# Transposing half of layer 1's rows in 32x32 blocks on VectorE, with a trip through DRAM, in place of TensorE

## The chip, the cores and the metric

One Trainium2 chip, one core. The metric is the device time of one execution in microseconds (us). The kernel before took 974.26 us (median of 3 runs, 972.87 to 974.94).

## The reference

The kernel computes two graph layers on 4096 rows of 512 numbers. Cut to what matters here:

```python
# layer 0: attention inside 32 graphs of 128 rows; adj is both bias and edge encoding
h = jnp.maximum(_layernorm(x, axis=-1), 0.0)
x = x + _L0_gnn_ref(h, adj, adj, ptr, Wq, bq, Wk, bk, Wv, bv)
# layer 1: graph attention over all 4096 rows, 8 heads of 64
h = jnp.maximum(_layernorm(x, axis=-1), 0.0)
mx = jnp.einsum('nf,hfd->hnd', h, W)          # projection
...
attn = jax.nn.softmax(jnp.where(adj[None] > 0, logits, neg_inf), axis=-1)
out_h = jnp.einsum('hij,hjd->hid', attn, mx)  # aggregation
x = x + ...
```

The change touches the rows of layer 1 between the norm and the projection. The projection needs each row tile (128 rows) transposed.

## The kernel before

Layer 0 writes its rows to `x1_d` in DRAM. For each of 32 row tiles, layer 1 loads the rows, norms them, transposes them with four TensorE matmuls, puts them through relu and projects them. Then it aggregates over all tiles with the masks in `a_d`.

```python
def norm(src, hn):
    nc.vector.bn_stats(stats, src)
    nc.vector.bn_aggr(mv, stats)
    nc.gpsimd.tensor_scalar(ve, mv[:, 1:2], EPS, None, ALU.add)
    nc.gpsimd.tensor_tensor(rstd, ve, neghalf, ALU.pow)                # L120
    nc.vector.tensor_scalar(hn, src, mv[:, 0:1], rstd, ALU.subtract, ALU.mult)   # L121

def relu_T(ps_pool, hn, dst):
    for k in range(KC):
        nc.tensor.transpose(pt[:, k, :], hn[:, ts(k, P)], ident)       # L127
    nc.scalar.activation(dst, pt, AF.Relu)                             # L128
...
def normed1(i):
    row = sb2.tile([P, D], F32, name="row1")
    nc.sync.dma_start(row, x1_d[i])
    norm(row, row)
    hT = sb2.tile([P, KC, P], F32, name="hT1")
    relu_T(ps_t, row, hT)
    return hT

def prepare(i, hT, part):
    pm = project1(ps_p, hT, w1x)                                       # L243, pp
    e = sb2.tile([P, EW], F32, name="e")
    nc.scalar.activation(e[:, ES:EC], pm[1][:, HW : HW + H], AF.Exp)
    weigh(e, pm)                                                       # L252, VectorE, frees PSUM
    split(e, part)                                                     # L231, GpSimd
...
for i in range(n - 1, NT):
    hT = nhT
    if i + 1 < NT:
        nhT = normed1(i + 1)
    prepare(i, hT, part_tile(lo if i < LO else hi, i))
# then, for every tile: mw load (L265), VectorE transpose (L270) and cast (L277) of the mask,
# and the aggregation pg (L283). After tile 1's: graphs_are_tiles (the check of ptr) and hold(...).
```

Some words used below: relu is max(x, 0). The *weighing* (`weigh`) multiplies the projected rows by e and so empties their PSUM tile. A *hand-off* is a point where one engine waits for a result of another. The *granted clock* is the share of its full speed that TensorE was given.

The order of each engine's instructions is fixed when the kernel is compiled, and it isn't the order of the program: the prediction names a mask load issued 127 us ahead of its use.

## Time and profile before

| | before |
|---|---|
| time, median | 974.26 us |
| span of the profiled execution | 970.5 us, granted clock 0.992 |
| projection of tile 5 starts (from about here on layer 1's rows set TensorE's pace) | 351.77 us |
| projection of tile 16 (the first that the change turns) | 405.14 us |
| aggregation (pg) starts | 468.74 us |
| aggregation lasts | 489.6 us |

I cut the stage at the starts of the projections of tiles 5 and 16 and of pg, read from TensorE's timeline. The *first stretch* (tile 5 to tile 16) takes 405.14 - 351.77 = 53.4 us, the *second* (tile 16 to pg) 468.74 - 405.14 = 63.6 us. The same cut is made for every kernel below. The profile lines of this kernel stand in the prediction.

### The profile page before, as it was taken

The page shows a single profiled execution, that of the slowest core. Times are in us where ns is not written, and L with a number is a line of the kernel's source. Part 1 is how long each engine was busy: PE and PEld are TensorE (multiplying, and loading weights), DVE is VectorE, ACT ScalarE, POOL GpSimd, SP SyncE. Part 2 cuts the span into 40 slices and gives each one's busy share as a digit, 9 for nine tenths or more (in the row PEclk, how much of TensorE's full clock was granted, in tenths as well). Part 3 has the DMA queues.
Part 4 walks back from the last instruction along what each step waited for, and adds up shares of the span by engine and source line. Part 5 has one row for each costly group of instructions (what it writes and reads, how often), then busy time and mean ns, then how long its engine had stood idle before and what let it go on. Part 6 is the DMA issues. An engine that isn't in the chain of part 4 may idle for free.

```text
span 970.5 us, 13180 instructions
## 1 busy us (share of the span) xinstructions
PE 940.3 (97%) x5051; PEld 817.5 (84%) x5051; DVE 459.4 (47%) x978; ACT 260.7 (27%) x505; POOL 184.0 (19%) x344
## 2 busy tenths in 40 slices
PE   8999999989999998999999999999999999999995
PEld 5676677766677776788999999999999999999994
DVE  4678777866766358655133242433424233242321
ACT  5865666665762222233100000000000000000000
POOL 2211113231122125555110110101011010110100
PEclk9999999999999999999999999999999999999998
DMA  9989889898883033221022312223131221312201
GB/s 343 419 346 378 322 329 364 355 369 317 336 339 148 33 104 108 72 66 55 1 76 56 88 50 82 62 69 87 44 87 52 80 85 47 87 49 82 61 27 37
DMA packets 58042, 148.28 MB, mean 153 GB/s; under 512 B 6386, under 2 KB 23026, under 8 KB 49778
## 3 DMA queue, kind: packets, MB, share of 16 engines
q1 hardware_dynamic: 48178, 130.31, 38.3%
q10 hardware_dynamic: 9792, 17.05, 4.6%
q8 instruction: 41, 0.67, 0.3%
q14 instruction: 31, 0.25, 0.1%
HBM read 113.77 MB, written 33.55 MB: 152 GB/s over the span
## 4 chain that ended last, share of the span: by engine, by line
PE 89%; DVE 3%; DMA 2%; POOL 2%; ACT 2%; issue 1%; SPq 0%; ACTq 0%; DVEq 0%; POOLq 0%
PE pg L283 50%; PE pp L420 11%; PE pp L408 10%; PE pp L243 9%; PE pp L493 3%; PE pss L466 3%; PE pt L127 2%; DMA row<-x_d 1%; POOL part L231 1%; DMA xg<-x 1%; DVE a L136 1%; ACT junk L443 1%; DVE row L121 0%; DVE stats L114 0%; POOL rstd L120 0%
## 5 line engine op out<-in xcount | busy, mean ns | idle before, releaser
L283 PE MATMUL pg<-part,at 128*128 128x348 f32 x3072 | 489.6, 321 | 1.2 <-DVE e L252 1.2
L283 PEld LDWEIGHTS pg<-part,at 128*128 128x128 f32 x3072 | 489.4, 188 | 1.5 <-issue 1.5
L277 DVE CAST at<-at 128x4096 fp32r<-128x4096 fp8e4 x32 | 74.0, 2313 | 312.2 <-PE pg L283 312.2
L290 ACT COPY tot<-pg 128x522 f32<-128x522 f32 x32 | 19.2, 599 | 470.5 <-PE pg L283 470.5
L443 ACT ACTIVATE junk<-a 128x2048 bf16<-128x2048 f32 (+15 forms) x92 | 124.4, 1352 | 48.7 <-DVE x L495 28.0
L243 PE MATMUL pp<-w1x,hT 128*128 128x256 f32 (+1 forms) x512 | 118.4, 385 | 0.0
L420 PE MATMUL pp<-wv,hT 128*128 128x512 f32 x256 | 116.6, 600 | 0.0
L408 PE MATMUL pp<-hT,m_sb 128*128 128x256 f32 x512 | 113.2, 379 | 0.0
L243 PEld LDWEIGHTS pp<-w1x,hT 128*128 128x128 f32 x512 | 95.7, 192 | 13.6
L408 PEld LDWEIGHTS pp<-hT,m_sb 128*128 128x128 f32 x512 | 96.1, 190 | 12.9 <-issue 0.5
L420 PEld LDWEIGHTS pp<-wv,hT 128*128 128x128 f32 x256 | 49.1, 192 | 61.9 <-issue 61.9
L136 DVE TENSOR_SCALAR a<-a 128x512 fp8e4<-128x512 f32 x256 | 98.2, 460 | 0.5 <-DMA a_d<-a 0.4
L595 POOL COPY den_all<-tot 128x1 f32<-128x1 f32 x31 | 5.8, 186 | 369.1 <-DVE tot L291 369.1
L128 ACT ACTIVATE hT<-pt 128x512 f32<-128x512 f32 x64 | 37.0, 598 | 68.8 <-PE pt L127 68.7
L604 POOL TENSOR_TENSOR tot<-tot,row 128x512 f32<-128x512 f32 x31 | 40.0, 1290 | 61.7 <-DVE tot L296 61.7
L231 POOL TENSOR_TENSOR part<-e,part 128x522 fp32r<-128x522 f32 x32 | 42.1, 1316 | 43.0 <-ACT part L230 38.8
L118 POOL TENSOR_SCALAR ve<-mv 128x1 f32<-128x1 f32 x64 | 18.7, 295 | 150.9 <-DVE mv L116 150.8
L252 DVE TENSOR_TENSOR e<-pp,e 128x256 f32<-128x256 f32 x64 | 26.6, 417 | 28.9 <-ACT e L371 25.2
L270 DVE STREAM_TRANSPOSE at<-mw 128x1024 f32<-128x1024 f32 x32 | 39.5, 1236 | 0.0
L120 POOL TENSOR_TENSOR rstd<-ve,neghalf 128x1 f32<-128x1 f32 x64 | 38.5, 604 | 4.4
L424 DVE TENSOR_TENSOR v<-pp,bv_sb 128x512 f32<-128x512 f32 x32 | 22.0, 688 | 36.0 <-PE pp L420 36.0
L412 ACT ACTIVATE gT<-pp,c_sb 128x256 f32<-128x256 f32 x64 | 29.7, 468 | 29.4 <-PE pp L408 29.3
(93 smaller groups left out, 584.1 us busy)
## 6 DMA issues: line engine op xcount, KB each, us to landing
a<-adj SPq DMA_DIRECT2D x64, 1024.0 KB, 13.1
a_d<-a SPq DMA_DIRECT2D x32, 512.0 KB, 10.6
row<-x_d SPq DMA_DIRECT2D x64, 256.0 KB, 3.5
mw<-a_d SPq DMA_DIRECT2D x128, 128.0 KB, 4.0
xg<-x SPq DMA_DIRECT2D x16, 512.0 KB, 4.7
x_d<-x ACTq DMA_DIRECT2D x32, 256.0 KB, 4.2
out<-tot ACTq DMA_DIRECT2D x31, 256.0 KB, 3.8
wkT_sb<-wkT SPq DMA_DIRECT2D x4, 256.0 KB, 6.3
```

The source lines that it names most:

```text
L120: nc.gpsimd.tensor_tensor(rstd, ve, neghalf, ALU.pow)
L128: nc.scalar.activation(dst, pt, AF.Relu)
L136: nc.vector.tensor_scalar(a8v[:, u], av[:, u], 0.0, None, ALU.is_gt, saturate=False)
L231: nc.gpsimd.tensor_sub(dst[:, :, 1, :], e3, dst[:, :, 0, :].bitcast(F32))
L243: nc.tensor.matmul(pm[g][:, :n], hT[:, k, :], w1x[:, k, g * HW : g * HW + n], start=(k == 0), stop=(k == KC - 1),)
L270: nc.vector.transpose(at8.rearrange("p c n b -> p (c n b)").bitcast(F32).rearrange("p (c u n) -> p c u n", c=NW, n=B), mw.rearrange("p u ( ...
L277: nc.vector.tensor_copy(at.rearrange("p (c b) q -> p c b q", b=BY), at8.rearrange("p c q b -> p c b q"))
L283: nc.tensor.matmul(pg[:, c, : 2 * CW1], at[:, j, :], part(j)[:, c].rearrange("p s w -> p (s w)"), start=(j == 0), stop=(j == NT - 1),)
L408: nc.tensor.matmul(pp[:, : G * P], m_sb[:, k, ts(m, P)], hT[:, k, :], start=(k == 0), stop=(k == KC - 1),)
L420: nc.tensor.matmul(pp, hT[:, k, ts(t, P)], wv[:, k, :], start=(k == 0), stop=(k == KC - 1))
L443: nc.scalar.activation(junk[:, c0:c1], a[:, c0:c1], AF.Exp, scale=2.0 * NEG, accum_out=sums[:, n : n + 1],)
L604: nc.gpsimd.tensor_add(num, num, row)
```

## The change

The intent is to take the transposes of tiles 16 to 31 off TensorE, which is full there. VectorE can transpose 32x32 blocks in SBUF, and it has time. The blocks then have to change partition groups. That is done by a write to DRAM and a read-back (the *trip*), four row tiles (a *group*) at a time. I call the norm, relu and block transpose of such a row its *turning*, and the number of tiles by which the program places it before its projection the *lead* (AHEAD). Cut to its core:

```diff
+MIXED = NT // 2
+AHEAD = 7
+    hT_d = dram.tile([NW, P, P // B, KC * P], F32, name="hT_d")
...
-        ptr_i = sb.tile([1, NPTR], I32, name="ptr_i", bufs=1)
+        ptr_i = sb.tile([1, NPTR], I32, name="ptr_i", tag="row3", bufs=1)
...
+            sb4 = prep.enter_context(
+                tc.tile_pool(name="sb4p", bufs=2, side="right", reuse_waits="tile")
+            )
+            def turn1(i):
+                row = sb4.tile([P, D], F32, name="row4", bufs=4)
+                nc.sync.dma_start(row, x1_d[i])
+                norm(row, row)
+                nc.scalar.activation(row, row, AF.Relu)
+                c, b = divmod(i, BY)
+                if b == 0:
+                    blocks[c] = sb4.tile([P, P // B, KC, BY, B], F32, name="blocks")
+                nc.vector.transpose(
+                    blocks[c][:, :, :, b], row.rearrange("p (k q f) -> p q k f", k=KC, f=B)
+                )
+                if b == BY - 1:
+                    nc.scalar.dma_start(hT_d[c], blocks[c].rearrange("p q k b r -> p q (k b r)"))
+                    hT = sb4.tile([P, P // B, KC, P], F32, name="hT4")
+                    for q in range(P // B):
+                        nc.sync.dma_start(
+                            hT[ts(q, B)].rearrange("p u k m -> p u (k m)"),
+                            hT_d[c, :, q].rearrange("(u f) w -> f u w", f=B),
+                        )
+                    mixed[c] = hT
...
             for i in range(len(ahead) - 1, NT):
+                if MIXED <= i + AHEAD < NT:
+                    turn1(i + AHEAD)
+                j = i + 1
+                if j < MIXED:
+                    hTs[j] = normed1(j)
+                hT = hTs[i] if i < MIXED else mixed[i // BY][:, i % BY]
                 prepare(i, hT, part_tile(lo if i < LO else hi, i))
```

The block trip mixes the rows of a group of four tiles, so half of the mask bytes of layer 0 are laid out in another order to match (one rearrange pattern), and so is the slow fallback path, which doesn't run here. The new buffer of ptr_i comes with the change: it makes the check of the pointer wait for row3, which is first used in the aggregation.

More of the change, by code (lines that the diff above doesn't have):

```diff
@@ L133, in mask_bytes @@
         a8v = a8.rearrange("p (u c q b) -> p u c b q", c=NW, q=B, b=BY)[:, :, half]
-        av = a.rearrange("p (c b u q) -> p u c b q", c=NW // 2, b=BY, q=B)
+        order = ("p (c b u q) -> p u c b q", "p (c u b q) -> p u c b q")[h]
+        av = a.rearrange(order, c=NW // 2, b=BY, q=B)
         for u in range(P // B):
@@ L566 @@
             )
-            n = len(ahead)
-            nhT = ahead[-1]
-            for i in range(n - 1, NT):
-                hT = nhT
-                if i + 1 < NT:
-                    nhT = normed1(i + 1)
+            sb4 = prep.enter_context(
+                tc.tile_pool(name="sb4p", bufs=2, side="right", reuse_waits="tile")
+            )
+            blocks, mixed = {}, {}
+            def turn1(i):
[18 more added lines that the diff above has]
+                    mixed[c] = hT
+            hTs = {len(ahead) - 1: ahead[-1]}
+            for i in range(len(ahead) - 1, NT):
+                if MIXED <= i + AHEAD < NT:
[4 more added lines that the diff above has]
+                hT = hTs[i] if i < MIXED else mixed[i // BY][:, i % BY]
                 prepare(i, hT, part_tile(lo if i < LO else hi, i))
@@ L828, with level_rows @@
                     tc.tile_pool(name="ps_m4", bufs=2, space=PSUM) as ps_m,
-                    tc.For_i(0, NT, 1) as i,
                 ):
-                    hT = sb.tile([P, KC, P], F32, name="hT1")
-                    row = load_row(sb, i)
-                    norm(row, row)
-                    relu_T(ps_t, row, hT)
-                    pm = project1(ps_m, hT, w1x)
-                    te = small.tile([P, H], F32, name="te")
-                    nc.vector.tensor_tensor(te, pm[1][:, HW : HW + H], shift, ALU.subtract)
-                    nc.vector.tensor_scalar(te, te, 0.0, None, ALU.min)
-                    e = sb.tile([P, EW], F32, name="e")
-                    nc.gpsimd.memset(e[:, EC:], 1.0)
-                    nc.scalar.activation(e[:, ES:EC], te, AF.Exp)
-                    weigh(e, pm)
-                    split(e, parts_e[:, ds(i, 1)].rearrange("p o c s w -> p (o c) s w"))
+                    def level_rows(i, row):
+                        hT = sb.tile([P, KC, P], F32, name="hT1")
+                        norm(row, row)
+                        relu_T(ps_t, row, hT)
+                        pm = project1(ps_m, hT, w1x)
+                        te = small.tile([P, H], F32, name="te")
+                        nc.vector.tensor_tensor(te, pm[1][:, HW : HW + H], shift, ALU.subtract)
+                        nc.vector.tensor_scalar(te, te, 0.0, None, ALU.min)
+                        e = sb.tile([P, EW], F32, name="e")
+                        nc.gpsimd.memset(e[:, EC:], 1.0)
+                        nc.scalar.activation(e[:, ES:EC], te, AF.Exp)
+                        weigh(e, pm)
+                        split(e, parts_e[:, ds(i, 1)].rearrange("p o c s w -> p (o c) s w"))
+                    with tc.For_i(0, MIXED, 1) as i:
+                        level_rows(i, load_row(sb, i))
+                    with tc.For_i(MIXED, NT, BY) as i:
+                        for u in range(BY):
+                            row = sb.tile([P, D], F32, name="row1")
+                            for b in range(BY):
+                                nc.sync.dma_start(
+                                    row[ts(b, B)],
+                                    x1_d[ds(i + b, 1), ts(u, B)].rearrange("o p d -> (o p) d"),
+                                )
+                            level_rows(i + u, row)
                 with (
```

## The prediction

> **What bounds the kernel now.** I read the page first: its chain of work that ended last, then the busy tenths, then windows over the stage that the change touches, the timeline of that stage, and its waits.
>
> ```profile
> PE 89%; DVE 3%; DMA 2%; POOL 2%; ACT 2%; issue 1%; SPq 0%; ACTq 0%; DVEq 0%; POOLq 0%
> ...
> L283 PE MATMUL pg<-part,at 128*128 128x348 f32 x3072 | 489.6, 321 | 1.2 <-DVE e L252 1.2
> ```
>
> TensorE carries 89% of the chain. Its largest group, the aggregation of layer 1 (pg), starts at 468.7 us and runs 489.6 us with an idle time of 1.2 us before it. The change removes nothing there. What it touches is the stage before: each of 32 row tiles of layer 1 is normed (VectorE, GpSimd), transposed by four TensorE matmuls into pt, passed through relu (ScalarE) and projected with w1x (pp, line 243). Counted from their starts in the timeline, tiles 16 to 31 are projected from about 404.5 us on, so I cut the stage there. Columns of the windows: stretch, its length, then busy time (instructions) of PE, weight loads, VectorE, ScalarE, GpSimd, then clock, DMA share and GB/s.
>
> ```profile
> 356.00:404.50 48.50, 42.92 (x200) 35.07 (x200) 37.90 (x76) 13.21 (x31) 26.08 (x48) 0.96 0.35 98
> 404.50:468.70 64.20, 63.06 (x318) 54.49 (x316) 33.92 (x79) 20.18 (x48) 34.52 (x75) 1.00 0.18 54
> ```
>
> In the second stretch TensorE is full (63.06 of 64.20) and VectorE has nearly half its time free. In the first, TensorE misses 5.6 us and VectorE is at 37.9 of 48.5. The timeline of TensorE in the full stretch (start, length, engine, line, count) gives the period:
>
> ```profile
> 448.11 0.60 PE L127 MATMUL pt<-ident,row 128*128 128x128 f32 x4
> 448.55 3.67 PE L243 MATMUL pp<-w1x,hT 128*128 128x264 f32 x16
> 452.06 0.60 PE L127 MATMUL pt<-ident,row 128*128 128x128 f32 x4
> 452.49 3.67 PE L243 MATMUL pp<-w1x,hT 128*128 128x264 f32 x16
> ```
>
> Start to start a tile takes 452.49 - 448.55 = 3.94 us: 3.51 of projection and 0.44 of transposes (448.55 - 448.11). The lengths overlap, so I use starts. The waits of TensorE from 350 to 475 us (waiter, released by: us, times, longest):
>
> ```profile
> PE pt L127 <- DVE row L121: 5.6, 4, 3.0
> PE pg L283 <- DVE e L252: 1.2, 1, 1.2
> ```
>
> So the only named waits are for a normed row, in the first stretch, and one for the last PSUM reader before the aggregation.
>
> **What the Trainium skill says.** "VectorE: DVE Perf Modes", section "The three transpose paths": VectorE only transposes 32x32 blocks and TensorE is the path for a whole 128x128. That is why the changed kernel needs a trip through DRAM to move blocks between partition groups. The kernel before already does this for the masks; its transposes of 128x1024 take 1236 ns (row below). "DMA: Bandwidth & Descriptors", section "Anatomy of one DMA" gives a fixed part of about 2.0 us and then bytes over 436 GB/s. That fit is for software-generated transfers; still, the shortest row load here takes 2.0 us and the median in this stage 2.6 us for 256 KB, close to its 2.6. The same page, "Two DMAs through the same engine are not ordered": a read of what another DMA wrote has to wait for its semaphore. So write and read-back add up; no run yet shows it for this pair. "SBUF — State Buffer", section "SBUF: two separate sides": VectorE and GpSimd can lock each other out of a shared port for a whole instruction. The trace agrees in kind: the norm of a row (L121) normally takes 0.55 us, but 1.44 us at 398.83, beside a GpSimd subtraction.
>
> **The change part by part.** The costs come from these groups (busy us, mean ns) and transfers (count, KB each, us to landing):
>
> ```profile
> L128 ACT ACTIVATE hT<-pt 128x512 f32<-128x512 f32 x64 | 37.0, 598 | 68.8 <-PE pt L127 68.7
> L252 DVE TENSOR_TENSOR e<-pp,e 128x256 f32<-128x256 f32 x64 | 26.6, 417 | 28.9 <-ACT e L371 25.2
> L270 DVE STREAM_TRANSPOSE at<-mw 128x1024 f32<-128x1024 f32 x32 | 39.5, 1236 | 0.0
> L120 POOL TENSOR_TENSOR rstd<-ve,neghalf 128x1 f32<-128x1 f32 x64 | 38.5, 604 | 4.4
> ...
> row<-x_d SPq DMA_DIRECT2D x64, 256.0 KB, 3.5
> mw<-a_d SPq DMA_DIRECT2D x128, 128.0 KB, 4.0
> wv<-wvT SPq DMA_DIRECT2D x1, 1024.0 KB, 7.4
> ```
>
> Removed: the transposes of 16 tiles on TensorE, 16 x 0.44 = 7.0 us, all in the stretch where TensorE is full. Busy time would say 64 matmuls x 0.28 = 18 us, or 10 us with their overlap taken out, but most of that is pipeline depth. Relu stays on ScalarE, from SBUF instead of PSUM; a 128x522 copy from SBUF takes 0.62 us against 0.60, so 16 times nothing.
>
> Added on VectorE: 16 transposes of 128x512, half of 1236 ns each, 16 x 0.62 = 9.9 us. Per tile VectorE does 0.69 + 0.18 (statistics) + 0.55 (norm) + 2 x 0.42 (weighing) = 2.26 us now. In the iterations that prepare tiles 16 to 24 it does 2.26 + 0.62 = 2.9 us within 3.51, so it fits. In iterations 9 to 15 it norms two tiles, 2 x 1.42 + 0.62 + 0.84 = 4.3 us against 3.94: over by 7 x 0.36 = 2.5 us. But this is the stretch where VectorE now also does other work. The check of the graph pointer (lines 304 to 330) takes 0.83 + 8 x 0.82 + 1.0 = 8.4 us, and three transposes and two casts of layer 1's masks take 3.7 + 5.2 = 8.9 us. The change puts ptr_i in the buffer of row3, which comes free only inside the aggregation, where VectorE is about 31% busy. The turning buffers (4 x 2 + 2 x 8 + 2 x 8 = 40 KB per partition) lie on the side where the mask buffers come next, which pushes those casts back too. So up to 17 us of VectorE work leaves the stretch and 7 to 10 turnings of 2.04 us come in. I book that as even.
>
> Added transfers: 4 writes of 1 MB and 16 reads of 256 KB, 8 MB in some 100 us, beside a DMA share of 0.18 to 0.35. Bandwidth is free; latency counts. For the last tile of a group: row load 2.6, norm 0.69 + 0.18 + 0.22 + 0.60 + 0.55 plus hand-offs of about 0.5 = 2.7, relu 0.6, transpose 0.62, write of 1 MB about 7 (the loads of 1 MB took 7.4 and 6.9), four reads together about 6 (estimate from 1 MB): 19.5 us. Its place in the program is four tiles ahead of the first use, 4 x 3.94 = 15.8 us or later 4 x 3.51 = 14.0 us. Taken in program order each group would be 4 to 5.5 us late. But the kernel before does not keep program order: the first mask loads of the aggregation are issued at 342.02 us, 127 us before their matmul, as soon as memory allows. The last rows of x1 leave for DRAM at 367.1 us, those of tiles 16 to 24 long before, and the turning needs only free buffers (four rows, two blocks). So I expect it to be drawn ahead by some tiles, and the groups to arrive mostly in time. I book 2 us of lateness in all.
>
> The switch into the aggregation keeps its 1.2 us; the first mask cast (2.3 us) has VectorE to itself in the last seven tiles, where only weighing is left. I book 0. The block order of half the mask bytes in layer 0 changes only strides, with runs of 32 floats as before: 0.
>
> Sum: -7.0 + 0 + 2 + 0 = -5 us; with a share of the 5.6 us of waits in the first stretch perhaps recovered, -6 us. 974.3 - 6 = 968 us.
>
> **Rivals.** *First, late groups.* The reads of a group wait on the SyncE queue for the write; any row load issued behind them waits too. For: that queue issues in order, the chain above is longer than its four tiles, and a late row blocks VectorE and then the weighing that frees PSUM. Against: the order is not the program's, and three of the four groups have rows loaded well ahead. With 5 us a group it makes 974 - 7 + 20 = 987 us; with rows blocked behind as well, about 1000. *Second, VectorE becomes the bound* in iterations 9 to 15, with the waits for GpSimd and ScalarE inside each norm in its order. For: it is at 37.9 of 48.5 there and TensorE already waits 5.6 us. Against: the pointer check moves out. It makes 972 to 980. *Third, more gain:* the moved pointer check and casts free the first stretch and its 5.6 us vanish with the 7.0: 961 to 963. *Fourth,* the first mask cast stands between the stages, since its buffers overlap the turning's: 2 to 6 us more, 970 to 974.
>
> **Range and chances.** The gain is capped: 7.0 + 5.6 = 12.6 us is 1.3%, so over 2% (19.5 us) faster needs something I do not see: 0.03. Over 2% slower needs 26 us of new waits, the strong form of the first rival: 0.10. The rest, 0.87, is within. The range goes from just below the third rival, 960, to a mild form of the first, 982; its upper side is longer because every surprise but one costs time.
>
> **What would show it.** Right: TensorE transposes of rows halve to 64; tiles 16 to 31 follow each other every 3.51 us; VectorE has 16 transposes of about 620 ns; the pointer check lies after 480 us; the aggregation starts some 6 us earlier and still takes 489 to 490 us. Wrong: TensorE waiting, every fourth tile, for a read of the turned rows (first rival); waits for the normed row above 8 us before tile 16 (second); a gap over 3 us before pg with a cast in it (fourth); transposes well over 620 ns, or writes over 10 us.

## The result, and the profile after

| | before | after |
|---|---|---|
| time, median of 6 runs | 973.04 us (972.23 to 974.94) | 984.65 us (983.46 to 988.76) |
| ratio of the fast runs | 1 | 1.0125 [1.0101, 1.0148] |
| profiled span, clock | 970.5 us, 0.992 | 981.6 us, 0.986 |

The kernel became 1.25% slower. That is inside the class "within 2%", but outside the range of 960 to 982, and the sign is wrong. Ratios here and below are the mean time of one kernel's fast runs over that of the other's fast runs of the same rounds, so not quite the ratio of the medians quoted.

Where the 11.1 us between the two profiled spans lie (starts read from TensorE's timeline; differences taken before rounding):

| part | before | after | difference |
|---|---|---|---|
| up to the projection of tile 5 | 351.8 | 351.0 | -0.8 |
| first stretch | 53.4 | 55.4 | +2.1 |
| second stretch | 63.6 | 73.05 | +9.5 |
| aggregation | 489.6 | 491.8 | +2.2 |
| rest | 12.2 | 10.3 | -1.9 |

The page of the kernel after, answering to the first two lines shown of before (chain by engine, and the aggregation's group):

```profile
PE 86%; DVE 5%; DMA 5%; POOL 2%; ACT 1%; issue 1%; SPq 0%; ACTq 0%; POOLq 0%; DVEq 0%
...
L288 PE MATMUL pg<-part,at 128*128 128x348 f32 x3072 | 491.8, 322 | 7.5 <-DVE at L282 7.5
```

TensorE's share of the chain fell, and VectorE and DMA now stand in it with 5% each. The aggregation waits 7.5 us for a mask cast where it waited 1.2 us. TensorE's waits in the stage (us, times, longest), after:

```profile
PE pg L288 <- DVE at L282: 7.5, 1, 7.5
PE pp L248 <- DMA hT<-hT_d: 7.4, 1, 7.4
PE pt L131 <- DVE row L125: 6.8, 4, 2.7
```

Before, there were 5.6 us for rows and 1.2 us ahead of pg. The two windows, after (the second runs to the new start of pg; columns as in the prediction):

```profile
356.00:404.50 48.50, 41.67 (x185) 33.74 (x184) 35.23 (x73) 15.30 (x34) 24.96 (x57) 0.93 0.44 134
404.50:479.50 75.00, 60.09 (x266) 51.25 (x265) 37.71 (x77) 18.51 (x43) 32.89 (x68) 0.93 0.42 114
```

Look at VectorE, the fifth figure. In the first window it is busy 35.2 us; before it was 37.9. So the busy time did come out even, as booked, and slightly better (over the whole first stretch 37.6 us after and 41.0 before). Yet TensorE ran 185 matmuls where it had run 200. TensorE's timeline shows how (start, length, engine, line, count, and the idle time before with its releaser):

```profile
369.82 3.67 PE L248 MATMUL pp<-w1x,hT 128*128 128x264 f32 x16
...
374.82 3.67 PE L248 MATMUL pp<-w1x,hT 128*128 128x264 f32 x16
380.80 1.12 PE L131 MATMUL pt<-ident,row 128*128 128x128 f32 x4 [2.31 <-DVE row L125]
381.71 4.78 PE L248 MATMUL pp<-w1x,hT 128*128 128x264 f32 x16
...
397.89 36.77 PE L248 MATMUL pp<-w1x,hT 128*128 128x264 f32 x160
442.05 29.93 PE L248 MATMUL pp<-w1x,hT 128*128 128x264 f32 x128 [7.39 <-DMA hT<-hT_d]
479.50 0.92 PE L288 MATMUL pg<-part,at 128*128 128x348 f32 x2 [7.52 <-DVE at L282]
```

The starts of the projections lie 374.82 - 369.82 = 5.0 us and 381.71 - 374.82 = 6.9 us apart instead of 3.94: tile by tile TensorE waits for a normed row. Part of the 6.9 us is a slower clock: the projection at 381.71 took 4.78 us instead of 3.67, and the granted clock was 0.52 from 382 to 384 us. After the wait of 2.71 us that ends at 397.25 it was 0.50 from 398 to 400 us. Later TensorE runs without transposes, ten tiles in one piece (160 matmuls) and then eight (128), but there is a hole between them, and another before pg.

**What VectorE does in a 5 us tile.** Its timeline, after:

```profile
371.75 0.66 DVE L118 BATCH_NORM_STATS2 stats<-row 128x6 f32<-128x512 f32 x1
372.83 1.44 DVE L125 TENSOR_SCALAR row<-row,mv,rstd 128x512 f32<-128x512 f32 x1 [0.42 <-POOL rstd L124]
...
375.36 0.55 DVE L125 TENSOR_SCALAR row<-row,mv,rstd 128x512 f32<-128x512 f32 x1 [1.00 <-POOL rstd L124]
375.82 0.42 DVE L257 TENSOR_TENSOR e<-pp,e 128x256 f32<-128x256 f32 x1
376.60 0.71 DVE L588 STREAM_TRANSPOSE blocks<-row 128x512 f32<-128x512 f32 x1 [0.36 <-ACT row L584]
```

and GpSimd's line of the same moment:

```profile
372.76 1.23 POOL L236 TENSOR_TENSOR part<-e,part 128x522 fp32r<-128x522 f32 x1
```

Two norms stand one after the other, one for TensorE's next tile and one for a turned tile. Each waits for GpSimd's rstd (0.42 and 1.00 us), and the first takes 1.44 us instead of 0.55 while GpSimd's split of 1.23 us runs beside it. Then the transpose waits 0.36 us for ScalarE's relu. None of these waits is long, but each holds up the whole list. From 350 to 410 us the norm's groups (busy us, mean ns, idle before) read, before:

```profile
L121 DVE TENSOR_SCALAR row<-row,mv,rstd 128x512 f32<-128x512 f32 x10 | 8.1, 805 | 7.4 <-POOL rstd L120 7.4
```

and after:

```profile
L125 DVE TENSOR_SCALAR row<-row,mv,rstd 128x512 f32<-128x512 f32 x15 | 12.5, 830 | 9.1 <-POOL rstd L124 6.7 <-POOL e L375 2.2
L588 DVE STREAM_TRANSPOSE blocks<-row 128x512 f32<-128x512 f32 x8 | 5.5, 695 | 1.1 <-ACT row L584 1.1
```

**The hole at 442.** The third group (tiles 24 to 27) is written, and read back, at these issue times of the ScalarE and SyncE queues:

```profile
429.07 0.36 ACTq L592 DMA_DIRECT2D hT_d<-blocks  x1
```

```profile
434.25 1.75 SPq L595 DMA_DIRECT2D hT<-hT_d  x4
```

From the write's issue to TensorE's start on it are 442.05 - 429.07 = 13.0 us. TensorE had finished the tiles before at 434.66 (397.89 + 36.77). So the last transpose of this group would have had to be done some 7 us earlier. Nothing of this group's last three rows had been drawn ahead: their loads were issued by 409.1 us and took at most 7.2 us, but VectorE began the first of them only at 419.56 and the last at 423.65 us, when TensorE was in tile 20, which is the last row's place in the program. From 412 to 419 us VectorE had only weighings in its list and waited 1.6 us for ScalarE before two of them. The fourth group, written at 442.26, was in time, but its read-back was issued only at 446.17; without this hole it would have been wanted near 434.66 + 4 x 3.51 = 448.7 us, so it probably owes its punctuality to the hole.

**The hole before pg.** VectorE's last steps, after:

```profile
472.37 0.18 DVE L313 CAST ends<-ends_i 1x64 f32<-1x64 int32 x1
...
475.46 0.42 DVE L624 TENSOR_REDUCE held<-ok 128x1 f32<-128x256 f32 x1
475.79 1.23 DVE L275 STREAM_TRANSPOSE at<-mw 128x1024 f32<-128x1024 f32 x1
477.06 2.29 DVE L282 CAST at<-at 128x4096 fp32r<-128x4096 fp8e4 x1
```

The last weighing, which starts at 472.02, ends about where this cut begins. After it come 475.79 - 472.37 = 3.4 us of checks (all but the first 0.1 us are the bound checks of `hold`) and then 1.23 + 2.29 us for the first mask, which in the kernel before was cast at 361.22 us. Its loads were issued at 342.02 us before and from 448.41 us on now.

### The profile page after: what moved, and what is told of

Its sections match the earlier page's. It is cut to its first block, busy times and chain, and to the rows that moved or that the text cites. A ratio compares the mean times of both kernels' runs of the same rounds, so it can differ in the third digit from the quotient of the medians.

```text
span 981.6 us, 13107 instructions
## 1 busy us (share of the span) xinstructions
PE 937.6 (96%) x4987; PEld 816.0 (83%) x4987; DVE 472.5 (48%) x994; ACT 261.0 (27%) x505; POOL 176.5 (18%) x344
## 4 chain that ended last, share of the span: by engine, by line
PE 86%; DVE 5%; DMA 5%; POOL 2%; ACT 1%; issue 1%; SPq 0%; ACTq 0%; POOLq 0%; DVEq 0%
PE pg L288 50%; PE pp L425 11%; PE pp L413 10%; PE pp L248 7%; PE pp L498 3%; PE pss L471 3%; DMA a<-adj 1%; DMA row<-x_d 1%; DVE row L125 1%; PE pt L131 1%; POOL rstd L124 1%; DVE stats L118 1%; DMA bv_sb<-bv 1%; DMA hT<-hT_d 1%; DMA hT_d<-blocks 1%
## 5 line engine op out<-in xcount | busy, mean ns | idle before, releaser
L288 PE MATMUL pg<-part,at 128*128 128x348 f32 x3072 | 491.8, 322 | 7.5 <-DVE at L282 7.5
L248 PEld LDWEIGHTS pp<-w1x,hT 128*128 128x128 f32 x512 | 99.2, 196 | 23.2 <-DVE e L257 7.8
L236 POOL TENSOR_TENSOR part<-e,part 128x522 fp32r<-128x522 f32 x32 | 39.7, 1240 | 42.1 <-ACT part L235 37.2
L122 POOL TENSOR_SCALAR ve<-mv 128x1 f32<-128x1 f32 x64 | 16.3, 259 | 157.9 <-DVE mv L120 157.7
L275 DVE STREAM_TRANSPOSE at<-mw 128x1024 f32<-128x1024 f32 x32 | 39.6, 1239 | 4.2 <-DMA mw<-a_d 4.2
L498 PE MATMUL pp<-v,sT 128*128 128x512 f32 x64 | 33.6, 607 | 2.7 <-ACT sT L492 2.4
```

The lines of the kernel that those rows point to most:

```text
L236: nc.gpsimd.tensor_sub(dst[:, :, 1, :], e3, dst[:, :, 0, :].bitcast(F32))
L248: nc.tensor.matmul(pm[g][:, :n], hT[:, k, :], w1x[:, k, g * HW : g * HW + n], start=(k == 0), stop=(k == KC - 1),)
L275: nc.vector.transpose(at8.rearrange("p c n b -> p (c n b)").bitcast(F32).rearrange("p (c u n) -> p c u n", c=NW, n=B), mw.rearrange("p u ( ...
L288: nc.tensor.matmul(pg[:, c, : 2 * CW1], at[:, j, :], part(j)[:, c].rearrange("p s w -> p (s w)"), start=(j == 0), stop=(j == NT - 1),)
L498: nc.tensor.matmul(po, sT[:, t, :], v, start=True, stop=True)
```

## The experiments

All eleven were run with three rounds against the kernel before (median 972.05 to 972.46 us in those rounds). "Stage" is first plus second stretch: 117.0 us before, 128.5 us after. It is read from one profiled execution, and executions of one kernel differ by 2 to 5 us, so I lean on stage differences where the ratio of the timed runs goes the same way.

### 1. no_transposes: the gain alone

The kernel before without the TensorE transposes of tiles 16 to 31. Its output is wrong, which doesn't matter for the time.

```diff
-                relu_T(ps_t, row, hT)
+                if i < NT // 2:
+                    relu_T(ps_t, row, hT)
+                else:
+                    nc.scalar.activation(hT.rearrange("p k m -> p (k m)"), row, AF.Relu)
```

> The kernel before with only the TensorE transposes of row tiles 16 to 31 left out: relu writes the untransposed row where the transposed one should be, so the result is wrong on purpose; loads, norms and projections stay. It measures what there is to gain. My step says 16 x 0.44 = 7.0 us: about 967 us, and a period of 3.51 us from tile 16 on. If VectorE or GpSimd were nearly the bound there (rival), the period stays above 3.6 us and the gain is under 4 us.

Measured: 968.85 us, ratio 0.9957 [0.9940, 0.9973], stage 111.5 us. The waits for rows stay (6.1 us), the one before pg is 1.9 us. What it shows: the main idea alone gives 0.43% of 972.5, about 4.2 us (3.6 by the medians, 5.5 by the stage of one execution), where 7.0 was booked. The 18 tiles without transposes took 64.95 us, so (64.95 - 3.67) / 17 = 3.60 us each and not 3.51. TensorE's weight loads waited 2.5 us in it for ScalarE's relu of a row. That lies at the border of the rival in my expectation: without the transposes, the engines that norm the rows are nearly the bound.

### 2. rows_act: is it the SyncE queue?

The kernel after, the loads of turned rows on ScalarE's queue instead of SyncE's, where they stood behind the read-backs.

```diff
-                nc.sync.dma_start(row, x1_d[i])
+                nc.scalar.dma_start(row, x1_d[i])
```

> The changed kernel with the loads of the rows to be turned issued from ScalarE's queue, so that they no longer stand behind a read-back that waits for its write on SyncE's queue. Queue theory: the 7.4 us wait of TensorE for the turned rows of the third group goes, the wait for the first mask cast (7.5 us) stays; 975 to 978 us. Rival, the trip through DRAM is itself too long for seven tiles of lead: the third group is still late by 5 us or more, 982 to 985. Rival, VectorE has too much to do: the wait stays and moves to normed rows, 982 or more.

Measured: 987.28 us, ratio 1.0142 [1.0117, 1.0168]. TensorE's waits:

```profile
PE pp L248 <- DVE e L257: 9.8, 6, 4.1
PE pg L288 <- DVE at L282: 7.5, 1, 7.5
```

The wait for turned rows is gone, and 9.8 us of waits for the weighing have come in its place: rows that arrived late (VectorE waited 5.3 and 6.0 us for two of them) now held up VectorE's list, and the weighing that frees PSUM stood behind them. In this kernel the queue decided the form of the wait and did not lower its cost. The simple queue theory fell.

### 3. mask_first and 4. first_act: what stands before pg?

mask_first gives the first mask load a buffer of its own, which the turning's buffers don't overlap:

```diff
+            mwp = straight.enter_context(
+                tc.tile_pool(name="mwp", bufs=1, side="right", reuse_waits="tile")
+            )
             for i in range(len(ahead) - 1, NT):
+                if i + AHEAD == NT - 1:
+                    mw0 = load_mask(mwp, 0)
```

> The changed kernel with the load of the first row tile's mask in a buffer of its own and placed ahead of the last two read-backs; its transpose and cast still use the memory of the turning. Memory theory (the cast waits until the turning's pool is given back): only the hold operations may step behind, the wait before the aggregation falls from 7.5 to 4.5 to 6 us, 982 to 984 us. Queue theory for this wait (the load was stuck behind the read-back): the wait falls to about 1 us, 978 us. The wait for the third group's turned rows stays at 7 us in both.

first_act goes further: the whole first mask, cast included, is made early in memory of its own. To find room, the turned rows share row1's buffers (loaded by ScalarE's queue) and there is one block buffer:

```diff
-                row = sb4.tile([P, D], F32, name="row4", bufs=4)
-                nc.sync.dma_start(row, x1_d[i])
+                row = sb2.tile([P, D], F32, name="row4", tag="row1")
+                nc.scalar.dma_start(row, x1_d[i])
-                    blocks[c] = sb4.tile([P, P // B, KC, BY, B], F32, name="blocks")
+                    blocks[c] = sb4.tile([P, P // B, KC, BY, B], F32, name="blocks", bufs=1)
+                if i == 24:
+                    at = load_mask(mwp, mwp, 0)
```

> The changed kernel with both: rows to be turned are loaded from ScalarE's queue (into the two row buffers that the normed rows use, one buffer of blocks instead of two), and the memory so freed holds the first mask's load, transpose and cast, which are done before tile 24. If the two waits are what made the change slower, both go: no wait over 1.5 us before the aggregation and none for turned rows over 2 us; 974 - 7 + about 2 = 966 to 970 us, faster than both kernels by a little. If the cause is the work on VectorE or the length of the trip, it stays above 976 us, and one block buffer makes that worse.

Measured: mask_first 983.99 us, ratio 1.0103 [1.0081, 1.0124]; its wait before pg:

```profile
PE pg L289 <- DVE held L630: 5.0, 1, 5.0
```

first_act 1011.15 us, ratio 1.0398 [1.0380, 1.0415], with these as its largest waits:

```profile
PE pt L131 <- DVE row L125: 18.9, 7, 7.5
PE pp L248 <- DVE e L257: 12.9, 4, 6.3
```

The wait before pg fell from 7.5 to 5.0 and, in first_act, to 0.6 us. In mask_first the loads of the first mask were issued from 351.58 us on, yet its transpose came only at 476.03 us, after the last weighing; the wait for the third group stayed, at 7.7 us. So memory is the cause of the late cast, as the memory theory said, and not the queue: the mask's buffers lie where the turning's are, and it can be made only when those come free. But first_act pays for that room with the turning's buffers, and its waits for rows nearly triple. Both waits that it was to remove are gone or small, and yet it takes 1011 us where I expected 966 to 970; as a remedy it is a bad bargain.

### 5. no_trip: what does the DRAM trip cost?

The kernel after without write and read-back; the projection reads the blocks directly (four block buffers). Its output is wrong, which doesn't matter for the time.

```diff
-                    nc.scalar.dma_start(hT_d[c], blocks[c].rearrange("p q k b r -> p q (k b r)"))
-                    hT = sb4.tile([P, P // B, KC, P], F32, name="hT4")
-                    for q in range(P // B):
-                        nc.sync.dma_start(...)
+                    hT = blocks[c].rearrange("p q k b r -> p q k (b r)")
```

> The changed kernel without the trip through DRAM: TensorE projects straight from the blocks that VectorE turned (four block buffers in the same memory), so the result is wrong on purpose; loads, norms, relu and VectorE transposes of the 16 tiles stay. If the trip is what makes groups late, directly or by holding up row loads behind it, no wait for turned rows over 1 us is left and only the wait for the first mask cast (7 us) remains: 970 to 976 us. If the work of turning on VectorE is the cost, waits on VectorE stay and it takes 980 us or more.

Measured: 980.87 us, ratio 1.0084 [1.0058, 1.0110]; stretches 56.0 and 69.15 us.

```profile
PE pt L131 <- DVE row L125: 10.3, 6, 2.3
...
PE pp L248 <- DVE e L257: 4.0, 4, 1.9
```

The wait of 7.5 us before pg is there as well. This is the second branch of my expectation: even with no trip at all the kernel is slower than before. The trip costs 128.5 - 125.15 = 3.3 us of the stage (by the ratios, 1.0084 against 1.0125, some 4 us, with intervals that just overlap); the larger part of the loss is not in it.

### 6. turn_unused: the turning alone

The kernel before, all TensorE transposes kept, with the whole turning and the new ptr_i buffer added and its result not used.

```diff
+                if MIXED <= i + AHEAD < NT:
+                    turn1(i + AHEAD)
                 if i + 1 < NT:
                     nhT = normed1(i + 1)
```

> The kernel before, with the changed kernel's turning, writes and read-backs added and their result unused; TensorE still transposes all tiles, so the result is right and TensorE never waits for turned rows. If only TensorE's wait for the turned rows were the trouble, the added cost is the first mask cast (6 us) and little else: 979 to 982 us. If the turning, standing in order on VectorE between the steps that TensorE needs, holds those up, it costs 15 us or more: 988 us or above, with waits for normed rows after tile 16 too, where the kernel before has none.

Measured: 1011.28 us, ratio 1.0405 [1.0381, 1.0428].

```profile
PE pt L130 <- DVE row L124: 30.4, 13, 6.3
```

TensorE never waits for the trip's data here, and has all its old work; it waits 30.4 us for rows where it waited 5.6. So the turning does harm without any wait for turned rows. How much of the 30.4 us is its place in VectorE's order can't be told from this run: its norms are additions here, as the old ones stay, and VectorE also waited 5.6 us for row loads. The wait before pg is only 1.1 us, presumably since nothing reads the turned rows, so that their memory comes free earlier.

### 7. ptr_only: the moved pointer check alone

The kernel before with that one line:

```diff
-        ptr_i = sb.tile([1, NPTR], I32, name="ptr_i", bufs=1)
+        ptr_i = sb.tile([1, NPTR], I32, name="ptr_i", tag="row3", bufs=1)
```

> The kernel before with only the pointer check moved out of the first stretch, by letting its buffer be row3's, as the change does. My third rival said that this frees VectorE there: waits for normed rows fall from 5.6 us to under 3 us and the time to 969 to 972 us. My booking as even needs at least a part of it. If it does nothing, 973 to 975 us, and the change got no relief from it.

Measured: 968.26 us, ratio 0.9962 [0.9944, 0.9980]; stretches 48.4 and 63.6 us. It is correct and beats both kernels, by a little more than I expected.

```profile
PE pt L127 <- DVE row L121: 2.5, 3, 1.9
```

So the relief that the prediction hoped for is real: 53.4 - 48.4 = 5.0 us of the first stretch, 3.8 us of the time. In the kernel after, the same line is there, and the first stretch takes 55.4 us. Against ptr_only the turning costs the first stretch 55.4 - 48.4 = 7.0 us.

### 8. ahead8 and 9. ahead5: more or less lead

```diff
-AHEAD = 7
+AHEAD = 8     # ahead8;  5 in ahead5
```

> The changed kernel with a lead of eight tiles instead of seven. If the trip is too long for the lead, 3.5 us more lead takes about that from the wait for turned rows (7.4 us): 978 to 982 us. If the order of the queues sets it, the wait changes with the order and not by 3.5 us; 980 to 990 us.

> The kernel after with AHEAD 5 instead of 7, right result: two turnings fewer stand before tile 14's projection. Theory (the turnings cost the first stretch in proportion, and the lead of the trip is too short anyway): first stretch 2 to 3 us shorter than 46.9, but the groups arrive 5 to 8 us later each where they were in time or late: PE waits for turned rows rise from 7.4 to 20-30 us in all; time 995-1010, ratio 1.023-1.038. Rival (the static order hides the program order, so AHEAD moves nothing but the first stretch): 981-985, ratio about 1.01.

Measured: ahead8 993.71 us, ratio 1.0224 [1.0206, 1.0242]; ahead5 990.65 us, ratio 1.0181 [1.0149, 1.0212]. TensorE's waits for rows and for turned rows, in us:

| AHEAD | waits for normed rows | waits for turned rows | sum |
|---|---|---|---|
| 5 | 5.3 | 14.8 | 20.1 |
| 7 (after) | 6.8 | 7.4 | 14.2 |
| 8 | 14.2 | 4.5 | 18.7 |

More lead moves turnings into the first stretch, where they delay rows; less lead makes the groups late. Seven is the best of the three tried (whether ahead5 is more than 2% slower stays unclear; six was not run), so the loss is hardly a badly chosen constant. In ahead8 the third group was in time and the fourth 4.5 us late; its time lies above both of my expectations. My expectation for ahead5 was too dark: the turned rows cost it 14.8 us and not 20 to 30, as two groups were late (3.1 and 11.7 us) and two in time.

### 10. direct_turn: the turned norm without GpSimd

The kernel after, but turned rows are scaled by their variance, which is near 1, so VectorE needs nothing from GpSimd for them. Wrong (relative error 0.057).

```diff
-                norm(row, row)
+                nc.vector.bn_stats(stats, row)
+                nc.vector.bn_aggr(mv, stats)
+                nc.vector.tensor_scalar(
+                    row, row, mv[:, 0:1], mv[:, 1:2], ALU.subtract, ALU.mult
+                )
```

> Wrong on purpose: the kernel after, but the turned rows are scaled by their variance (near 1) instead of its inverse root, so the 16 turned norms no longer wait for the two GpSimd steps; statistics, norm, relu, transposes, trip and buffers stay. Theory (VectorE bound by ordered hand-offs in the first stretch): the group of norms waiting for GpSimd shrinks, the stretch up to the projection of tile 14 falls from 46.9 us by 3 to 5 us, the wait of PE for rows from 6.8 to 2-3 us, the groups also come 1-3 us earlier, and the time lies near 977-981 (ratio 1.004-1.008). Rival (VectorE is short of plain instruction time, or the port contention of the norm itself sets it): the stretch stays within 1.5 us of 46.9 and the ratio stays at 1.011-1.013. The boundary before the aggregation stays at 7-8 us in both.

Measured: 979.52 us, ratio 1.0076 [1.0045, 1.0108]; stretches 57.8 and 65.2 us. TensorE's timeline from tile 15 on:

```profile
400.69 0.66 PE L131 MATMUL pt<-ident,row 128*128 128x128 f32 x4 [4.14 <-DVE row L125]
403.02 48.39 PE L248 MATMUL pp<-w1x,hT 128*128 128x264 f32 x208 [1.67 <-ACT hT L132]
452.55 14.27 PE L248 MATMUL pp<-w1x,hT 128*128 128x264 f32 x64 [1.15 <-DVE e L257]
474.33 2.08 PE L288 MATMUL pg<-part,at 128*128 128x348 f32 x6 [7.52 <-DVE at L282]
```

The stage is 128.5 - 123.0 = 5.5 us shorter (by the ratios some 4.8 us, with intervals that just overlap), and the ratio is what the ordered hand-offs were expected to give. Up to tile 14 the stretch did shrink, from 46.9 to 41.6 us, as expected. But the compiled order changed with the edit: more turnings were drawn ahead of tile 15, whose row then came late (4.14 us), so the first stretch up to tile 16 grew by 2.4 us. The net gain is in the second: every group is in time, with no wait for turned rows. VectorE and the trip did the same work otherwise; only 32 small GpSimd instructions and the waits for them are gone. That does not show that the hand-offs made the third group late. Its write was issued at 417.61 us instead of 429.07, and in act_norm below, where the hand-offs stay in another place, it was issued at 416.04: the changed order is as good an explanation.

### 11. act_norm: norm and relu of turned rows on ScalarE

A right result: rows are normed and put through relu in one ScalarE instruction, so VectorE has 16 norms fewer.

```diff
-                norm(row, row)
-                nc.scalar.activation(row, row, AF.Relu)
+                # stats, mv, ve and rstd as in norm
+                nc.gpsimd.tensor_scalar(nb, mv[:, 0:1], rstd, -1.0, ALU.mult, ALU.mult)
+                nc.scalar.activation(row, row, AF.Relu, bias=nb, scale=rstd)
```

> A right result: the kernel after, but the turned rows are normed and put through relu in one ScalarE instruction (scale rstd, bias -mean*rstd from one more small GpSimd step), so VectorE keeps only statistics and transpose for them and never waits for rstd of a turned row. Theory (ordered hand-offs on VectorE): the first stretch falls by 3 to 6 us from 46.9, some of it given back because the transpose still waits in order for ScalarE; time 976-981, ratio 1.004-1.008. Rival (plain instruction time on VectorE of the transposes, or the added GpSimd step): little change, ratio 1.010-1.014. It should not beat the kernel before by 2% in either.

Measured: 984.10 us, ratio 1.0113 [1.0084, 1.0143]; stretches 58.9 and 69.6 us. My expectation of 976 to 981 us missed, though up to tile 14 the stretch fell from 46.9 to about 41.5 us, as expected; then tile 15's row came 4.3 us late. The group of transposes from 350 to 410 us:

```profile
L597 DVE STREAM_TRANSPOSE blocks<-row 128x512 f32<-128x512 f32 x9 | 6.4, 708 | 10.8 <-ACT row L593 10.8
```

VectorE has less to do, and now waits 10.8 us in front of nine transposes, 1.2 us each, for ScalarE's instruction that waits for GpSimd. The wait was moved from the norm to the transpose and stayed in the same list. So VectorE's busy time is not the price: over the stage it fell from 74.9 to 60.5 us, and the stage stayed at 128.5 us. In direct_turn it hardly fell (72.9 us), and the stage became 5.5 us shorter. In both the compiled order changed too, so that what the hand-offs alone are worth is not shown.

## Why the prediction was wrong

The failed step is this one: **"So up to 17 us of VectorE work leaves the stretch and 7 to 10 turnings of 2.04 us come in. I book that as even."** As a statement on busy time it was right (35.2 us after, 37.9 before, in the same window). As a statement on TensorE's time it was wrong. Of the work that left, the pointer check was worth 5.0 us of the stretch (ptr_only); the mask casts still stood there in ptr_only, where TensorE's waits for rows were only 2.5 us, so their going could bring little more. The turnings that came in are chains across VectorE, GpSimd, VectorE, ScalarE and VectorE, and each of their waits holds up whatever stands behind it, the norms and weighings that TensorE needs among it. They cost 7.0 us of the first stretch against ptr_only. These come out of the two timelines: 6.8 - 2.5 = 4.3 us more waits for rows, and 3.2 us of slower clock after two of these waits (from 380.80 to 386.32 us and from 397.25 to 406.45 TensorE did in 14.7 us what takes 11.5 at full pace; ptr_only has nothing of the kind), less 0.9 for two transposes that are gone: 6.6 of 7.0.

Step by step:

- **Removed transposes, -7.0 us.** Right in kind: 18 tiles in a row then follow each other without them. In size too large: alone it brought about 4.2 us of time (no_transposes), where the rows no longer quite kept up (3.60 us a tile and not 3.51). In the second stretch itself, 16 tiles at 3.51 us take 56.2 us where the kernel before needed 63.6 less its wait of 1.2, so 6.2 us were freed there and spent again.
- **VectorE even, 0.** Failed, as above. The transposes also took 695 ns and not 620.
- **Lateness of the groups, 2 us.** It was 7.4 us, in one group. The sum for write and read-back was right, 13 us booked and 13.0 measured, with some luck: the write took 5.1 us and not 7, the rest 7.9 and not 6. What failed is the hope that the turning would be drawn ahead enough: the first two groups were in time, but the third ran in its place in the program, for which the prediction itself had worked out 4 to 5.5 us of lateness. It came 7.4 us late. Two kernels whose compiled order drew this group ahead (direct_turn, act_norm) had it in time; why it wasn't drawn ahead here is not shown. By the stage of no_trip the trip cost 3.3 us in all.
- **Boundary, 0.** It was 7.5 - 1.2 = 6.3 us, and mask_first and first_act confirm what the fourth rival said, that the mask's buffers overlap the turning's. I had seen that the turning's memory "pushes those casts back" and counted it as a relief for the first stretch. I didn't follow where they would land. Of the 7.5 us, 3.4 are bound checks that stand before the mask in VectorE's order.
- **What no step contained: the clock after a hole.** Besides the 3.2 us in the first stretch (the kernel before had 1.4 there): the 128 matmuls after the wait at 442 took 29.93 us; eight tiles at the full pace take 7 x 3.51 + 3.67 = 28.24. So the hole cost 1.7 us on top of its own length, and the aggregation, which starts after the other hole, took 2.2 us more than before. The Trainium skill, "TensorE: Matmul & The Clock Gate", section "What's actually happening", says that the clock halves after an idle window of about 3.4 us and comes back after as long a busy one; that would make 1.7 us a hole (an estimate from the page), and for the two long holes this trace agrees: the granted clock was 0.50 from 440 to 444 us and from 478 to 482 us. But in the first stretch gaps of 2.31 and 2.71 us, shorter than such a window, were followed by half the clock as well, while one of 3.02 us in no_transposes was not; here the length of a gap alone did not decide it.

The second stretch adds up: -6.2 for 14 of the tiles (the transposes of two lie before the cut; 14 x 0.44), +7.4 for the turned rows, +1.7 for the clock, +6.3 at the boundary, in all +9.2 of the 9.5 us measured.

Of the rivals, the first came true in one group of four, the fourth in full (6.3 us), and the third as far as the moved pointer check frees time. Of the second, the longer first stretch came true, but the waits for rows stayed at 6.8 us, under the 8 us that were to show it. I had priced each on its own, starting from the full gain of 7.0 us, and drawn the range over these single outcomes. Their sum lies outside it. The sum shouldn't have been a surprise: all of them follow from one fact, that the turning's work and memory come to lie between things that TensorE is waiting for.

What stays open: how the 4.3 us of added waits in the first stretch divide between VectorE's waits for GpSimd, the norms that take 1.44 us beside GpSimd's split, and plain added work. Every edit also changes the compiled order, so no run here isolates one of them. Nor was it tried to move only the 3.4 us of checks behind the first mask.

## What to carry to other kernels

Before moving work to an engine that has time, count not only its busy time but the hand-offs in the new work: where the order is fixed, each wait for another engine delays everything behind it, and what stands behind it may be what the busiest engine needs next. Count a wait of the busiest engine at more than its length, too, if its clock falls after it, as it did here. Follow memory as well as time: ask for each new buffer what was prefetched into that place before, and where that will land now. And undo the parts of a change one by one; here a line that came along with it (ptr_only, 0.38% faster than before) was worth keeping, and the main idea was not.

## What the Trainium skill lacked or had wrong

- "VectorE: DVE Perf Modes", section "The three transpose paths", gives one figure for VectorE, for 128x128 in bf16. It has none for fp32 or for blocks written with strides. Here 128x512 fp32 into strided blocks took 695 ns (mean of 8), where half of the masks' 128x1024 (1239 ns, so 620) was booked. Halving was the error: if both layouts cost alike, the second 512 elements added 1239 - 695 = 544 ns, so that some 151 ns belong to each of these transposes, whatever its length (an estimate from these two). This is said of that section, not of the rest of the page.
- None of the pages drawn on here warns that a gap in an engine's order, and not its busy time, is the price of moved work. The runs: VectorE's busy time fell from 37.9 to 35.2 us in the window while TensorE's matmuls in it fell from 200 to 185, and taking 16 norms off VectorE (act_norm) left the stage at 128.5 us.
- "TensorE: Matmul & The Clock Gate", section "What's actually happening", does not say what gaps shorter than its window do. Here half the clock followed gaps of 2.31 and 2.71 us (0.52 from 382 to 384 us, 0.50 from 398 to 400 us) and did not follow one of 3.02 us in no_transposes (1.00 from 380 to 386 us).
